# A decoder layer whose side work is placed by an account of the engines' time, with keys in column parts and FFN weight chunks converted on ScalarE

## The chip, the core and the metric

The kernel runs on one core of one Trainium2 chip. A core has TensorE (PE in the profile, its weight loads PEld), VectorE (DVE), ScalarE (ACT), GpSimd (POOL) and SyncE (SP, which here only issues DMAs). The results of matmuls lie in PSUM tiles, from which VectorE and ScalarE read them. The metric is the time of one execution in microseconds on the device. It was 1882.19 us before the change, the median of three runs from 1882.07 to 1885.43.

## What is computed

The input is x of 16 sequences, 256 positions and 512 columns, with a context of the same shape. Three sublayers are added to it in turn, each behind a layer norm:

```python
x = x + mamba2(layernorm(x))       # W_in 512 -> 2048 z + 2048 x + 64 B + 64 C + 32 dt
x = x + xattn(layernorm(x), ctx)   # linear attention over 16 heads
x = x + ffn(layernorm(x))          # 512 -> 2048 (gate, up) -> 512, ternary weights, int8 activations
# mamba2, per head: h[t] = exp(A dt[t]) h[t-1] + dt[t] x[t] B[t];  y[t] = C[t] h[t] + D x[t]
#   x, B, C go through a causal convolution of 4 taps and silu; y * silu(z); RMS norm; @ W_out
# xattn: qh = sigmoid(q wq + bq); kh = sigmoid(ctx wk + bk); vh = ctx wv + bv
#   kv[h] = sum over positions of kh * vh; state = cumsum(kv over heads); (qh * state) @ wo + bo
# ffn: weights rounded to -1, 0, 1 by the mean of their absolute values; activations to 8 bits
```

## The kernel before

The 16 sequences go in 8 pairs. The 2048 inner columns of the mamba sublayer are 16 units of 128 columns (two heads). One pair and one unit make a **slot**; 128 slots follow one another and are written out by hand in a loop over `s`, which interleaves three units: in slot s, unit s is projected, unit s-1 gets its recurrence, unit s-2 its output product. The main instructions of a slot, by tile name and line of the kernel before:

- TensorE: the projection Z (12 matmuls into `pp`, L676) with four transposes `trx` of unit s-1 in its middle (L941), the projection X (12 more `pp`), the recurrence as matmuls `py` of unit s-1 (L961, L968), the output product `po` of unit s-2 (12 matmuls, L1011).
- VectorE: `times_g` on `m` of unit s-1 (L929, L933), two scans into `m` of unit s (L912), three taps of the convolution into `xs` (L693), `y` of unit s-1 (L976, L981).
- ScalarE: eight `xdt` copies (L951), `zs` (L891), `yh` (L987), the start of the convolution `xs` (L897), `sq` (L998), four `m` (L920), silu of `xs` (L906).
- GpSimd: `yl` (L988), which the output product needs, and `ssq` (L999).

Z and X go into two PSUM buffers in turn (pool `ps_p`, tag `proj`). Z is let go by `zs`, X by the last tap.

All else is a **side step** of a generator (a `Task` in the list `beside`): the layer norm of the next pair (`norm_pair`), its time steps dt and decays (`time_steps`, L700 to L775: tiles `sp_*`, `dt`, `da`), its B and C (`states`: `bc`, `bcT`, `pg`, `g`), the context (`context_pair`: `pk`, `kh`, `ptt`, `ptk`; `context_group`: `kv`, `zp`), the attention of pairs already finished (`batch_end`: `q`, `pa`), and the preparation of the FFN weights (`ffn_sums`, `ffn_quantised`: 48 chunks of 128x512, two passes). A slot has eight moments (`POINTS`). A generator yields what its next step needs (engine, microseconds, allowed moments, moments to wait) and `due` lets it go when the moment is allowed and the microseconds given out on that engine since the last reset stay under `room` (2.3 on VectorE, 2.5 on ScalarE, 2.0 on TensorE, 2.5 on GpSimd). Steps that empty a PSUM bank (`leaves`) go in any case.

A side product on TensorE needs a bank (`Banks.take`): at moment 3, between X and `py`, it takes the buffer of Z ("z"); at moment 7, behind `po`, a bank of its own ("own"). With "z" the two buffers change places: the next Z then waits for the last tap of this slot's X, and no longer the next X.

The order of the instructions on each engine is the order in which the program writes them: no scheduler changes it. The same holds for the DMAs on the queues of SP and POOL. Behind the last slot comes the FFN: 32 tiles of 128 rows, 48 matmuls each, with the last batches' attention beside it.

In the context, keys of two batches go through `pk` (four column tiles, L1225), then four matmuls with `kp` stationary and the 16 columns of `pick` moving (L1246), a copy to SBUF (L1250), a tanh (L1253), a scaling (L1255); the sums over positions `ptt` (L1264) are copied (L1270), turned by four matmuls with a 128x32 selection matrix `sel` (L1277) and copied out (L1289, L1293). An FFN chunk is scaled and rounded on ScalarE (L1474), clipped on VectorE (L1476), brought to bfloat16 on GpSimd (L1480) and stored by GpSimd's DMA queue (L1486).

## Time and profile before

| what | value |
|---|---|
| median of three runs | 1882.19 us |
| the profiled execution | 1887.88 us |
| its span, first to last instruction | 1886.1 us |
| granted TensorE clock, mean | 0.986 |
| busy: PE, DVE, ACT, POOL | 95%, 87%, 66%, 36% of the span |
| slots 2 to 17 | from 52 to 260 us |
| slots 18 to 126 | from 260 to 1512 us |
| last slot and FFN | from 1512 to 1886 us |

Each time in the profile is from the span's start. A row gives line, engine, operation, the tiles written and read, and shapes. In the view of waits a row says which engine stood idle in front of which instruction, who released it, and then the sum, the number of times and the longest. In a timeline a row is start, duration, instruction, and in brackets the idle time in front of it.

The slots' limits in the table are starts of the first matmul of a Z in the timeline of TensorE.

### The profile page before, as it was taken

How to read it: one execution, taken by the hardware profiler on the slowest of the kernel's cores; microseconds unless marked ns; L12 is line 12 of the kernel's file. 1: busy time of each engine (PE TensorE's matmuls, PEld its weight loads, DVE VectorE, ACT ScalarE, POOL GpSimd, SP SyncE). 2: the span in 40 equal slices, each digit the busy share in tenths (PEclk: the TensorE clock that was granted, in tenths of full speed). 3: DMA queues.
4: the chain of work that ended last, by engine and by line, in shares of the span. 5: the costliest groups of instructions: out<-in, count | busy, mean ns of one | idle time of the engine just before them, and what ended most of it. 6: DMA issues, size and time to landing. Idle time of an engine off the chain costs nothing.

```text
span 1886.1 us, 30373 instructions
## 1 busy us (share of the span) xinstructions
PE 1786.5 (95%) x10464; PEld 1018.1 (54%) x10464; DVE 1638.2 (87%) x2711; ACT 1248.1 (66%) x2896; POOL 682.2 (36%) x691
## 2 busy tenths in 40 slices
PE   6789999998999998999999999998999989999998
PEld 4445555555556555555555555565656544444443
DVE  6989888777888889888988998989887888999997
ACT  5777666675666666666666666666666557777775
POOL 1233432344434354546454636463533222211000
PEclk8999999999999999999999999999999999999999
DMA  5764776788768777877597879787867734655454
GB/s 163 240 185 136 235 191 174 217 257 223 168 196 270 201 196 235 258 192 191 185 268 211 199 205 252 202 193 186 238 188 213 250 89 99 133 123 130 108 120 95
DMA packets 296933, 358.95 MB, mean 190 GB/s; under 512 B 163765, under 2 KB 197861, under 8 KB 296778
## 3 DMA queue, kind: packets, MB, share of 16 engines
q1 hardware_dynamic: 277962, 296.13, 60.0%
q0 software_dynamic: 18240, 60.84, 9.4%
q8 instruction: 83, 1.36, 0.3%
q14 instruction: 72, 0.59, 0.1%
q10 hardware_dynamic: 576, 0.04, 0.0%
HBM read 279.70 MB, written 39.58 MB: 169 GB/s over the span
## 4 chain that ended last, share of the span: by engine, by line
PE 57%; DVE 25%; DMA 7%; ACT 5%; issue 4%; POOL 2%; SPq 1%; ACTq 0%; POOLq 0%; DVEq 0%
PE pp L676 21%; PE po L1011 11%; PE po_f L1621 5%; PE pg L1579 4%; PE pu L1579 4%; DVE m L912 4%; DVE xs L693 4%; PE py L961 4%; DVE m L929 2%; PE trx L941 2%; DMA w<-w_d 2%; PE py L968 2%; DVE m L933 1%; DVE sp_q L742 1%; DVE y L976 1%
## 5 line engine op out<-in xcount | busy, mean ns | idle before, releaser
L676 PE MATMUL pp<-lnT_h_m,w 128*128 128x512 f16 (+1 forms) x2056 | 661.1, 383 | 23.3 <-DVE xs L693 20.8
L676 PEld LDWEIGHTS <-w 128*128 128x128 f16 x3084 | 296.5, 99 | 364.3 <-issue 35.8
L988 POOL TENSOR_TENSOR yl<-y,yh 128x512 fp32r<-128x512 f32 x128 | 178.9, 1398 | 717.5 <-ACT yh L987 659.3
L693 DVE SCALAR_TENSOR_TENSOR xs<-pp,convw_sb,xs 128x510 f32<-128x510 f32 (+2 forms) x384 | 286.1, 745 | 151.1 <-ACT xs L897 141.6
L676 PE MATMUL pp<-lnT_l_m,w 128*128 128x512 f16 (+1 forms) x1028 | 393.4, 383 | 0.0
L1011 PE MATMUL po<-wout,yh 128*128 128x512 f32 x1024 | 337.0, 410 | 4.6 <-DMA wout<-wout_d 4.6
L951 ACT ACTIVATE xdt<-trx,dt 128x64 f32<-128x64 f32 x1024 | 223.5, 328 | 167.4 <-PE trx L941 167.3
L912 DVE TENSOR_TENSOR_SCAN m<-dab,starts 128x512 f32<-128x512 f32 x254 | 302.2, 1230 | 0.5 <-DMA dab<-da_d 0.5
L1011 PEld LDWEIGHTS po<-wout,yh 128*128 128x128 f32 x1024 | 183.8, 189 | 61.3 <-issue 15.1
L1011 PE MATMUL po<-wout,yl 128*128 128x512 f32 x512 | 203.7, 398 | 3.0 <-POOL yl L988 3.0
L906 ACT ACTIVATE xs<-xs 128x512 f32<-128x512 f32 x128 | 80.9, 632 | 186.3 <-DVE xs L693 186.3
L961 PE MATMUL py<-m,xdt 128*64 128x256 f32 x1024 | 162.1, 395 | 11.1 <-DVE m L933 5.2
L1579 PEld LDWEIGHTS <-yT 128*128 128x128 bf16 x1024 | 100.0, 98 | 131.1 <-issue 14.7
L920 ACT ACTIVATE m<-edb,m 128x128 f32<-128x128 f32 x508 | 162.7, 395 | 12.1 <-DVE m L912 12.1
L999 POOL TENSOR_TENSOR ssq<-ssq,sq 128x512 f32<-128x512 f32 x120 | 158.6, 1321 | 27.9 <-ACT sq L998 27.0
L897 ACT ACTIVATE xs<-pp,convb_sb,convw_sb 128x512 f32<-128x512 f32 x128 | 100.3, 783 | 102.2 <-PE pp L676 102.1
L929 DVE TENSOR_TENSOR m<-m,g 128x1024 f32<-128x1024 f32 x128 | 161.9, 1265 | 0.1
L1579 PE MATMUL pg<-w_ffn,yT 128*128 128x512 bf16 x512 | 132.3, 381 | 4.7 <-ACT h L1583 4.7
L1579 PE MATMUL pu<-w_ffn,yT 128*128 128x512 bf16 x512 | 132.3, 381 | 4.6 <-DVE x L1037 4.6
L1621 PE MATMUL po_f<-w_ffn,hT 128*128 128x512 bf16 x512 | 125.4, 379 | 2.0 <-DMA hT<-hq 2.0
L1583 ACT ACTIVATE h<-pg,sg 128x512 f32<-128x512 f32 x128 | 86.6, 683 | 51.6 <-PE pg L1579 51.3
L1011 PEld LDWEIGHTS po<-wout,yl 128*128 128x128 f32 x512 | 96.7, 189 | 29.7 <-POOL yl L988 6.4
(278 smaller groups left out, 2791.9 us busy)
## 6 DMA issues: line engine op xcount, KB each, us to landing
dab<-da_d SPq DMA_DIRECT2D x127, 512.0 KB
wout<-wout_d SPq DMA_DIRECT2D x112, 512.0 KB
edb<-ed_d SPq DMA_DIRECT2D x127, 256.0 KB
w<-w_d SPq DMA_DIRECT2D x40, 512.0 KB
raw<-in_w_zx SPq DMA_DIRECT2D x16, 512.0 KB
wout_d<-wout SPq DMA_DIRECT2D x16, 512.0 KB
ctxT<-in_ctx_t POOLq DMA_DIRECT2D x16, 512.0 KB, 7.8
x<-in_x SPq DMA_DIRECT2D x16, 512.0 KB
```

The lines of the kernel that those rows point to most:

```text
L676: nc.tensor.matmul(dst, w(wi, kc), yT[yi][:, :, kc, :], start=n == 0, stop=n == 3 * KD - 1)
L693: nc.vector.scalar_tensor_tensor(u[:, :, d:S], raw[:, :, 0 : S - d], w[:, j : j + 1], u[:, :, d:S], ALU.mult, ALU.add,)
L912: nc.vector.tensor_tensor_scan(u["m"][:, 4 * j : 4 * j + 4, :].rearrange("p k t -> p (k t)"), u["da"][j].rearrange("p h i t -> p (h i t)") ...
L920: nc.scalar.activation(u["m"][:, 8 + n, :], u["ed"][:, n // 2, n % 2, :], AF.Copy, scale=u["m"][:, 2 * n, P - 1 : P],)
L929: nc.vector.tensor_tensor(m, m, gi.unsqueeze(2).to_broadcast([P, 2, 2, NT * P]), ALU.mult)
L951: nc.scalar.activation(u["xdt"][:, j, i, h, :], u["tr"][:, j, i, h * HD : (h + 1) * HD], AF.Copy, scale=dt[:, i, j, 2 * c + h : 2 * c + h ...
L961: nc.tensor.matmul(py[h * HD : (h + 1) * HD, j, :].rearrange("p (i t) -> p i t", i=NT), xdt[:, j, 0, h, :], m[:, 2 * (2 * j + h) : 9 + 2 * ...
L988: nc.gpsimd.tensor_tensor(lo, u["y"], hi, ALU.subtract)
L999: nc.gpsimd.tensor_tensor(pair["ssq"], pair["ssq"], sq, ALU.add)
L1011: nc.tensor.matmul(pair["po"][n], u["yhl"][yi][:, j, i * P : (i + 1) * P], w[:, wi, :], start=c == 0 and p == 0, stop=c == NU - 1 and p == 2,)
L1579: nc.tensor.matmul(dst, yT[:, kc, :], w_ffn[w + kc][:, cols], start=kc == 0, stop=kc == KD - 1)
L1621: nc.tensor.matmul(u["po"], u["hT", k // (KF // 2)][:, k % (KF // 2), :], w_ffn[2 * KD + k // NF][:, (k % NF) * D : (k % NF + 1) * D], sta ...
```

## The change

1. **The account.** A `Model` holds one running time per engine. Every main instruction of a slot and every side step adds its microseconds there, behind what it depends on; VectorE steps that read two SBUF tensors and GpSimd steps push each other back. From slot 18 on, `due` no longer goes by `room`: a step goes when its input is ready by the account and `fits` says that the taps (VectorE), the `xdt` copies (ScalarE) or GpSimd's times would not come later than the account has TensorE needing them, plus a slack that grows with the step's delay and, from five slots before its deadline, with its urgency. `Banks.take` asks the same before a side product. Waits between steps of a task are cut to one moment.
2. **Order.** Norm, time steps and states of the next pair but one start one slot earlier (`AHEAD` 4 for 3).
3. **Keys.** `pick` (now 128x32) is stationary and `kp` moves, in four column tiles; the tanh reads PSUM; one transpose (`pk3`) turns the result; the scaling reads it from PSUM. The sums `ptt` are laid out by halves of the columns so that two transposes replace the four matmuls with `sel`; the copies out double. `pg` is two matmuls (256 and 128 columns) instead of three.
4. **FFN chunks.** The copy to bfloat16 is a ScalarE activation; the store stays on GpSimd's DMA queue, at least four moments later.

The diff, cut to its core (the calls `model.op(...)` behind each main instruction, with its microseconds, are left out, and the `us=` given to each `bank.take`):

```diff
+class Model:
+    def __init__(self):
+        self.t = dict.fromkeys(("pe", "act", "dve", "pool"), 0.0)
+        self.port, self.pool = [], []
+        self.proj, self.turn = [0.0, 0.0], 0
+        self.tp = 0.0
+    def op(self, engine, us, *after, port=False):
+        start_ = max([self.t[engine]] + [a + 0.1 for a in after])
+        if port:
+            for a, b in self.pool[-6:]:
+                if a <= start_ < b:
+                    start_ = b
+                    break
+            self.port.append((start_, start_ + us))
+        elif engine == "pool":
+            for a, b in self.port[-8:]:
+                if a < start_ < b:
+                    start_ = b
+                    break
+            self.pool.append((start_, start_ + us))
+        self.t[engine] = start_ + us
+        return start_ + us
+    def bank(self):
+        self.turn = 1 - self.turn
+        return 1 - self.turn
+    def convolved(self, dve, x_end):
+        return max(dve, max(x_end, self.t["act"]) + 0.9) + 2.3
...
+    def urgent(self, task):
+        return 0.5 * max(0, clock[0] / POINTS - task.deadline + 5)
+    def fits(self, task, moment, us):
+        t, e = self.t, task.engine
+        slack = 0.3 + 0.25 * max(0, clock[0] - task.due) / POINTS + self.urgent(task)
+        if e == "dve":
+            if moment < 3:
+                taps = self.convolved(t["dve"] + us, t["pe"] + X_US)
+                end = t["pe"] + X_US + Y_US + OUT_US
+            else:
+                taps = self.convolved(
+                    t["dve"] + us + G_US + SCAN_US, t["pe"] + X_US + Z_US
+                )
+                end = t["pe"] + Z_US + X_US + Y_US + OUT_US
+            return taps <= end + slack
+        if e == "act":
+            return t["act"] + us <= t["pe"] + Z_US / 2 + 0.8 + slack
+        if e == "pool":
+            return t["pool"] + us <= t["pe"] + (5.0 if moment > 3 else 9.0) + slack
+        return True
+Z_US, X_US, Y_US, OUT_US, G_US, SCAN_US = 3.1, 2.6, 1.5, 2.85, 1.9, 2.45
+model = Model()
+current = [None]
+def modelled():
+    return (NU + 2) * POINTS <= clock[0] < NP * NU * POINTS
...
+    def take(self, own=False, first=False, us=None, leaves_us=0.7):
         me = [own]
+        task = current[0]
+        us = us or (task and task.pe_us) or 0.3
         self.line.insert(0 if first else len(self.line), me)
+        asked = clock[0]
+        def fits():
+            if not modelled():
+                return True
+            t, slack = model.t, 0.3 + 0.25 * (clock[0] - asked) / POINTS
+            slack += model.urgent(task)
+            if task.ready > t["pe"] + slack:
+                return False
+            if clock[0] % POINTS == 3:
+                taps = model.convolved(t["dve"], t["pe"])
+                return taps <= t["pe"] + us + Y_US + OUT_US + slack
+            taps = model.convolved(
+                t["dve"] + leaves_us + G_US + SCAN_US, t["pe"] + us + Z_US + X_US
+            )
+            return (
+                self.free_at <= t["pe"] + slack
+                and taps <= t["pe"] + us + Z_US + X_US + Y_US + OUT_US + slack
+            )
         while True:
             moment = clock[0] % POINTS
             if steady() and moment == 3:
                 others = [one for one in self.line if not one[0]]
-                if self.free["z"] and others and others[0] is me:
+                if self.free["z"] and others and others[0] is me and fits():
                     hold = "z"
                     break
             elif self.free["own"] and self.line[0] is me and (
-                not steady() or moment == 7 and clock[0] >= self.since
+                not steady() or moment == 7 and clock[0] >= self.since and fits()
             ):
                 hold = "own"
                 break
             yield WAIT
         self.line = [one for one in self.line if one is not me]
         self.free[hold] = False
+        if task and steady():
+            after = [task.ready]
+            if hold == "z":
+                self.z = model.bank()
+                after.append(model.proj[self.z])
+            else:
+                after.append(self.free_at)
+            task.ready = model.op("pe", us, *after)
...
-        for n, (s0, t0) in enumerate(((0, 0), (P, P), (0, P))):
+        for n, (s0, t0, t1) in enumerate(((0, 0, S), (P, P, S))):
             nc.tensor.matmul(
-                pg[:, n, :], bcT[0:NS, j, s0 : s0 + P], cT[:, j, t0 : t0 + P],
-                start=True, stop=True,
+                pg[:, 2 * n : 2 + n, :].rearrange("p n t -> p (n t)"),
+                bcT[0:NS, j, s0 : s0 + P], cT[:, j, t0:t1], start=True, stop=True,
             )
         yield leaves(dve(0.7))
         nc.vector.tensor_tensor(
-            g[:, j, 0:2, :], pg[:, 0:2, :], upper.unsqueeze(1).to_broadcast([P, 2, P]),
+            g[:, j, 0:2, :], pg[:, 0:3:2, :], upper.unsqueeze(1).to_broadcast([P, 2, P]),
             ALU.mult,
         )
-        nc.vector.tensor_copy(g[:, j, 2, :], pg[:, 2, :])
+        nc.vector.tensor_copy(g[:, j, 2, :], pg[:, 1, :])
...
         yield moved(1.3, 1)
         ct.append(q2.tile([P, NT, D], F32, tag="ctx", name=f"ctx_{b + k}"))
         nc.gpsimd.dma_start(ct[k], cx[b + k].rearrange("(i p) d -> p i d", p=P))
     yield pe(0.2, 1)
-    hold = yield from bank.take()
-    pk = misc(hold, [P, 2, NT, H], f"pk2_{b}")
-    for k in range(2):
-        for i in range(NT):
-            nc.tensor.matmul(
-                pk[:, k, i, :], kp[:, k, i * P : (i + 1) * P], pick, start=True, stop=True
-            )
-    yield leaves(dve(0.1))
-    nc.vector.tensor_copy(kh[:, :, :, 0:H], pk)
-    bank.give(hold)
-    yield act(0.1)
-    nc.scalar.activation(kh[:, :, :, 0:H], kh[:, :, :, 0:H], AF.Tanh, scale=0.5)
-    yield dve(0.1)
-    nc.vector.tensor_scalar(
-        kh[:, :, :, 0:H], kh[:, :, :, 0:H], 0.5, 0.5, ALU.mult, ALU.add
-    )
-    yield pe(0.5)
-    hold = yield from bank.take()
-    pt = misc(hold, [P, D], f"ptt_{b}")
+    hold = yield from bank.take(us=0.35)
+    pk = misc(hold, [P, P], f"pk2_{b}")
     for k in range(2):
         for i in range(NT):
             r = 64 * k + 32 * i
             nc.tensor.matmul(
-                pt[r : r + 32], kh[:, k, i, :], ct[k][:, i, :],
+                pk[r : r + 32], pick, kp[:, k, i * P : (i + 1) * P],
                 start=True, stop=True, tile_position=(0, r),
             )
-    yield leaves(dve(0.6))
-    tt = q1.tile([P, D], F32, tag="ttT", name=f"ttT_{b}")
+    yield leaves(act(0.3, 2))
+    khT = q1.tile([P, P], F32, tag="khT", name=f"khT_{b}")
+    nc.scalar.activation(khT, pk, AF.Tanh, scale=0.5)
+    bank.give(hold)
+    yield pe(0.2, 2)
+    hold = yield from bank.take(us=0.15)
+    pk = misc(hold, [P, 2, NT, 32], f"pk3_{b}")
+    nc.tensor.transpose(pk.rearrange("p k i h -> p (k i h)"), khT, ident)
+    yield leaves(dve(0.1))
+    nc.vector.tensor_scalar(
+        kh[:, :, :, 0:H], pk[:, :, :, 0:H], 0.5, 0.5, ALU.mult, ALU.add
+    )
+    bank.give(hold)
+    yield pe(0.5)
+    hold = yield from bank.take(us=1.0)
+    pt = misc(hold, [P, 2, P], f"ptt_{b}")
+    for i in range(NT):
+        for n in range(2):
+            for k in range(2):
+                r = 64 * n + 32 * k
+                nc.tensor.matmul(
+                    pt[r : r + 32], kh[:, k, i, :],
+                    ct[k][:, i, :].rearrange("p (j n d) -> p n j d", j=2, n=2)[:, n],
+                    start=i == 0, stop=i == NT - 1, tile_position=(0, r),
+                )
+    yield leaves(dve(0.4))
+    tt = q1.tile([P, 2, P], F32, tag="ttT", name=f"ttT_{b}")
     nc.vector.tensor_copy(tt, pt)
     bank.give(hold)
     yield pe(0.2)
     j = b % NG
-    hold = yield from bank.take()
-    pt = misc(hold, [P, KD + 1, 4, 2, 4], f"ptk_{b}")
-    for kc in range(KD):
-        nc.tensor.matmul(
-            pt[:, kc].rearrange("p q k h -> p (q k h)"), tt[:, kc * P : (kc + 1) * P],
-            sel.rearrange("p q k h -> p (q k h)"), start=True, stop=True,
-        )
+    hold = yield from bank.take(us=0.6)
+    pt = misc(hold, [P, 2 * P + 2 * H], f"ptk_{b}")
+    for n in range(2):
+        nc.tensor.transpose(pt[:, n * P : (n + 1) * P], tt[:, n], ident)
+    sums = pt[0:1, 2 * P :].rearrange("p (k q h) -> p k q h", k=2, h=4)
     for k in range(2):
         for i in range(NT):
             nc.tensor.matmul(
-                pt[0:1, KD, :, k, :], ones[:, 0:1],
+                sums[:, k], ones[:, 0:1],
                 kh[:, k, i, 0:H].rearrange("p (q h) -> p q h", h=4),
                 start=i == 0, stop=i == NT - 1,
             )
-    yield leaves(dve(0.2))
-    nc.vector.tensor_copy(
-        group["tt"][:, :, :, j : j + 2, :].rearrange("p c q k h -> p (c q) (k h)"),
-        pt[:, 0:KD].rearrange("p c q k h -> p (c q) (k h)"),
-    )
-    nc.vector.tensor_copy(group["ksum"][:, :, j : j + 2, :], pt[0:1, KD])
+    yield leaves(dve(0.3))
+    turned_ = pt[:, 0 : 2 * P].rearrange("p (c k q h) -> p c k q h", c=KD, k=2, h=4)
+    for k in range(2):
+        nc.vector.tensor_copy(
+            group["tt"][:, :, :, j + k, :], turned_[:, :, k, 0:4]
+        )
+        nc.vector.tensor_copy(group["ksum"][:, :, j + k, :], sums[:, k])
     bank.give(hold)
     ctxs.give()
     paired.add(b)
...
         yield dve(0.5)
         nc.vector.tensor_scalar(t, t, MAGIC + 1.0, MAGIC - 1.0, ALU.min, ALU.max)
         yield from q8s.take()
-        yield pool(1.3)
+        yield act(0.65)
         q = q2.tile([P, 512], BF16, tag="wq8", name=f"wq8_{k}")
-        nc.gpsimd.tensor_scalar(q, t, -MAGIC, None, ALU.add)
+        nc.scalar.activation(q, t, AF.Copy, bias=-MAGIC)
         chunks.give()
+        yield issued()
         if w < 2:
             dst = (wg_d, wu_d)[w][:, n // NF, (n % NF) * 512 : (n % NF + 1) * 512]
         else:
...
 def due(task, now):
     if now < task.due or now % POINTS not in task.points:
         return False
+    if task.engine and task.engine != "dma" and modelled():
+        if task.engine == "pe":
+            if task.ready > model.t["pe"] + 0.3:
+                return False
+            task.pe_us = task.us
+        else:
+            if not task.must and (
+                task.ready > model.t[task.engine] + 0.2
+                or not model.fits(task, now % POINTS, task.us)
+            ):
+                return False
+            task.ready = model.op(task.engine, task.us, task.ready, port=task.port)
+        task.engine = None
+        return True
+    if modelled() and not task.engine and task.ready > model.t["pe"]:
+        return False
+    if task.engine == "pe":
+        task.pe_us = task.us
     if task.engine:
         used = spent.get(task.engine, 0)
         scarce = (first_room if now < (NU + 2) * POINTS else room)[task.engine]
...
+                    task.port = task.engine == "dve" and not must
+                    if modelled() and task.engine and task.engine != "dma":
+                        wait = min(wait, 1)
+                    elif not task.engine and wait > 4:
+                        task.ready = 0.0
...
-    if (s == 1 or c == NU - 3) and k + ahead < NP:
+    if (s == 1 or c == NU - AHEAD) and k + ahead < NP:
         pair = pairs[k + ahead] = {"k": k + ahead}
-        start(s, norm_pair(pair), rank=-4)
-        start(s, time_steps(pair), rank=-1 if k else -5)
-        start(s, states(pair), rank=-1)
+        first = (k + ahead) * NU
+        start(s, norm_pair(pair), rank=-4, deadline=first - 11)
+        start(s, time_steps(pair), rank=-1 if k else -5, deadline=first - 3)
+        start(s, states(pair), rank=-1, deadline=first)
...
-            start(s, batch_end(batches[2 * ended["k"] + j]), rank=2)
+            start(s, batch_end(batches[2 * ended["k"] + j]), rank=2, deadline=s + 12)
```

## The prediction

> **What bounds the kernel now.** I read the page first, for shares; then the starts of the matmuls, slot by slot; then the stretches between slots; then the waits of TensorE inside the slots; last one disturbed place in the timelines.
>
> ```profile
> PE 1786.5 (95%) x10464; PEld 1018.1 (54%) x10464; DVE 1638.2 (87%) x2711; ACT 1248.1 (66%) x2896; POOL 682.2 (36%) x691
> ...
> PE 57%; DVE 25%; DMA 7%; ACT 5%; issue 4%; POOL 2%; SPq 1%; ACTq 0%; POOLq 0%; DVEq 0%
> ```
>
> TensorE is the bound, and VectorE is close enough behind it to hold it up now and then: 25% of the chain that ended last runs through VectorE.
>
> ```profile
> core 0: us, PE busy (x) PEld busy (x) DVE busy (x) ACT busy (x) POOL busy (x), PEclk, DMA share, GB/s
> 0.00:260.00 260.00, 218.92 (x1243) 129.49 (x1244) 222.99 (x367) 169.88 (x397) 77.34 (x94) 0.95 0.65 193
> 260.00:1512.00 1252.00, 1210.52 (x7527) 723.31 (x7523) 1078.12 (x1558) 822.38 (x2160) 554.53 (x539) 0.99 0.77 213
> 1512.00:1886.00 374.00, 357.08 (x1703) 165.30 (x1701) 337.06 (x787) 255.81 (x340) 50.32 (x58) 1.00 0.50 112
> ```
>
> The account works in the second row alone (slots 18 to 126). The first is unmodelled; the last has 1536 FFN matmuls 0.216 us apart, 332 of its 374 us, and the built order of the changed kernel differs there by one late `pa`. So the row to cost is 1252 us, 109 slots.
>
> By the starts of the matmuls a slot with no side product takes 10.08 us (slots 28 to 31, each 10.07 to 10.09): 24 `pp` at 0.216, 12 `po` at 0.235, `py` 1.45, `trx` 0.44. 109 x 10.08 = 1099, so 153 us are on top. The side products at the price of their undisturbed groups: `pk`, `pk2`, `ptt`, `ptk` 1.00, 0.81, 1.08, 1.14, seven times, 28; `bc` with `pd` 3.79, `pda` 0.25, two `pg` 1.93, six times, 36; `kv`, `stp`, `zp` 2.57, four times, 10; `pq` 0.85, six times, 5; `q`, `q_t` and two `pa` 1.24, fourteen times, 17. Together 97. The rest, 56 us, is stall. Of it TensorE's waits in this stretch name 41, these five and six under 1.7:
>
> ```profile
> PE pp L676 <- DVE xs L693: 20.2, 12, 3.4
> PE py L961 <- DVE m L933: 4.6, 5, 1.1
> PE po L1011 <- DMA wout<-wout_d: 4.6, 2, 4.3
> PE trx L941 <- ACT xs L906: 3.3, 4, 1.3
> PE pk L1246 <- DVE kp L1231: 2.4, 1, 2.4
> ```
>
> Half of the named stall is one event twelve times over: Z waits for the last tap of the slot before. Here is the longest:
>
> ```profile
> 1271.97 1.25 DVE L735 TENSOR_SCALAR sp_s<-sp_v 128x128 f32<-128x128 f32 x1
> 1273.25 0.95 DVE L736 RECIPROCAL sp_s<-sp_s 128x128 f32<-128x128 f32 x1
> ...
> 1275.03 2.30 DVE L693 SCALAR_TENSOR_TENSOR xs<-pp,convw_sb,xs 128x510 f32<-128x510 f32 x3
> ```
>
> ```profile
> 1273.55 0.40 PE L1122 MATMUL pa<-z,q 96*128 96x512 f32 x1
> 1277.39 0.39 PE L676 MATMUL pp<-lnT_h_m,w 128*128 128x512 f16 x1 [3.44 <-DVE xs L693]
> ```
>
> Five time-step instructions stood ahead of the taps, and a `pa` in Z's buffer had made the next Z wait for those taps. Either alone does less harm: without the side product Z takes the buffer that `zs` freed and only X, 3.1 us later, needs the taps. The account's `fits` tests exactly this pair.
>
> **The change, part by part.** The sum is made against the profiled execution, 1887.9 us. Two rows of the groups (busy time and mean ns of one behind the bar) price the moved copy: as it is on GpSimd, and the same shape on ScalarE.
>
> ```profile
> L1480 POOL TENSOR_SCALAR wq<-wchunk 128x512 bf16<-128x512 f32 x48 | 77.0, 1604 | 2.9 <-DVE wchunk L1476 2.9
> ...
> L1555 ACT ACTIVATE yq<-y 128x512 bf16<-128x512 f32 x32 | 20.1, 629 | 43.2 <-DVE y L1547 43.2
> ```
>
> *TensorE's own work.* The four `pk2` groups of a pair take 0.81 to 0.89 (eight passes 0.112 apart, and the way out). Four column tiles are shown by `pk` (L1225): its four tiles start 0.007 apart, the rounds of 256 columns 0.195 to 0.22. One round pair of 128 columns is 0.22, plus 0.1 going in (0.31 to 0.33 from the matmul before, where untiled groups have 0.22) and 0.1 going out: 0.42. The new transpose costs 0.26 (`pda`). 0.68 for 0.85: -0.17. `ptk`'s turning goes from eight passes (0.90) to four (0.44 and 0.1 out): -0.36. `ptt` stays: twice the matmuls, half the columns. `pg` loses one weight load and keeps its columns, 0.86 to about 0.78. 8 x 0.53 + 16 x 0.08 = -5.5; bounds 0 (the new handshake PSUM, ScalarE, TensorE, VectorE eats it) and -9 (a round as cheap as the 0.007 spacing suggests).
>
> [...] The trace shows some 0.2 us for going in and out. [...]
>
> *The account.* 41 us of stall are named. The DMA rows (`wout` 4.6, the streamed `w` 1.5) are not its business: 35 left. It is blind in one place that I can price: `time_steps` declares 1.2 us for five instructions that take 0.23 + 0.95 + 0.29 + 0.29 + 0.23, at least 2.0 and in the timeline above 3.1; and 1.7 for nine that take 9 x 0.29 = 2.6, in slot 104 4.7 with GpSimd beside them. That is about 2 us too little, in each of the six pairs from slot 18 on: 12 us that I leave standing. 35 - 12 = -23. Bounds: 0, and -43 (all 35 and half of the 16 unnamed). I take the value nearer the middle since the gaps of over 2 us lie both in time-step slots (56, 72, 89, 104) and elsewhere (34, 40, 57).
>
> *What it adds.* Held to the account, VectorE's side work comes in bundles. From the built order and the rows' medians, slots with over 4 us of it rise from 5 to 14; slots 71 and 88 get 7.6 each (time steps and a norm). A slot frees about 2 us of VectorE (10.1 less 8.1 for scans, taps, products), so such a bundle is late by up to 5.5. What hides it: neither has a side product in Z's buffer, and the slots behind them have 0.2 and 0.7 us. If that cover is gone, see the third rival.
>
> *FFN chunks.* GpSimd loses 48 x 1.60 = 77 us. On VectorE, 14 instructions beside `wq` lasted 4.9 us longer than their quickest kind: at most that comes back. Eight transposes on SP (L652) waited 11.8 us for GpSimd behind `wq`; SP queues the decay loads behind them, but TensorE waited for no `dab`. -1, bounds -5 and 0. ScalarE gains 48 x 0.63 (the row of `yq`, 128x512 f32 to bfloat16, 629 ns): 30 us, on an engine busy 822 of 1252. Behind the new copy queue `xdt` and `zs`, for which `py` and the buffer wait. Main work takes 6.4 of a 10.8 us slot, so 4.4 are free; by the built order five slots exceed that (40, 69, 73, 83, 104), by 3.6 in all, before by none. +3, bounds 0 and 30 (every copy in front of an `xdt` that TensorE needs). The chunk's store stands on GpSimd's queue ahead of `yl`; it is issued half a slot behind the copy, so it finds it done: 0.
>
> *Moved steps.* Norm, time steps and states start a slot earlier, with, for each pair, the loads of x and four transposes, `cT`, and the stores of `da` and `ed`, past one slot's `dab`, `edb` and `wout` on SP. The stores land earlier than needed; a transpose that waits on GpSimd could hold a `wout`: 0, bounds 0 and 4.3 (the `wout` row). The small copies (`kh` two for one, `ttT` half as wide, `tt` and `ksum` doubled) change VectorE by -1 us over all pairs: 0.
>
> Sum: -5.5 - 23 - 1 + 3 = -26.5; 1861.4 against 1887.9, and by 1882.19 / 1887.88 that is **1856** on the median.
>
> **The rivals.** *The account takes nearly all.* Slack hides the undercount too; 43 + 5.5 + 1 go: 1834. For it: most stalls are pairings that it tests. Against: six under-declared steps. *The stalls only move.* The account's clock is not the chip's (GpSimd stretches VectorE's steps, weights and DMAs aren't in it), old stalls go and as many come; 5.5 us of products and little more remain: 1876. For it: the `room` rule already left some 80 of the 109 slots without a stall over 0.3 us. *Bundles on VectorE stall TensorE: slower.* Each of the 14 slots waits for what exceeds 4 us (2 free, 0.9 of side products, 1.1 before Z needs the taps): 22 us by the built order, 3 before. With none of the old stall gone that is +19 - 5.5: 1896. It decides where less than 14 us of old stall goes. Against: eleven of the 14 have a slot with under 1.1 us beside them.
>
> **How the numbers follow.** Forecast 0.47 (1842 to 1872), nearly all 0.15, moved 0.18, bundles 0.20. No change is within 0.2%, 3.8 us, about what a measurement of this kernel can tell. Faster: 0.47 + 0.15 + 0.15 of the third = 0.77; same 0.05; slower 0.18. The range 1830 to 1892 leaves out a few hundredths below and the worse half of the bundles above.
>
> **What would show it.** Right: slots 18 to 126 in some 1226 us; `pp <- xs` under 10; waits left in the slots of `sp_s` and `sp_q`; `wq` rows on ACT at 0.63, none on POOL; `pk2` and `pk3` together 0.7. Wrong: `pp <- xs` at 20 or more, or waits at slots 71 and 88 over 3 us (bundles); `py <- xdt` and `pp <- zs` growing (ScalarE); a span of the first 18 slots other than 260 us.

## The result, and the profile after

The changed kernel takes 1935.79 us (median of 4 runs, 1930.6 to 1939.71) against 1882.86 (4 runs) before: a ratio of 1.027, 95% interval 1.0242 to 1.0297. The forecast was 1856. The page of the changed kernel, the shares of its engines and of the chain that ended last:

```profile
PE 1789.3 (92%) x10456; PEld 1013.2 (52%) x10456; DVE 1626.3 (84%) x2717; ACT 1274.7 (66%) x2944; POOL 602.4 (31%) x642
...
PE 54%; DVE 21%; ACT 8%; DMA 7%; issue 6%; POOL 3%; SPq 1%; ACTq 0%; POOLq 0%; DVEq 0%
```

TensorE is as busy as before (1789 us for 1787) in a longer span. VectorE's part of the chain fell from 25% to 21%; ScalarE's rose from 5% to 8%. The same three stretches as in the prediction (start and end, length, busy time by engine, granted clock, DMA share):

```profile
core 0: us, PE busy (x) PEld busy (x) DVE busy (x) ACT busy (x) POOL busy (x), PEclk, DMA share, GB/s
0.00:261.00 261.00, 215.59 (x1255) 127.51 (x1255) 221.80 (x366) 170.47 (x397) 77.98 (x94) 0.95 0.64 193
261.00:1563.00 1302.00, 1214.36 (x7506) 719.64 (x7499) 1068.60 (x1571) 848.59 (x2209) 473.52 (x490) 0.98 0.74 205
1563.00:1938.00 375.00, 359.34 (x1704) 166.07 (x1702) 335.91 (x782) 255.65 (x339) 50.90 (x58) 0.99 0.50 113
```

All the loss lies in slots 18 to 126: 1302 us for 1252, where 1226 was forecast. TensorE's waits in that stretch (total, times, longest):

```profile
PE pp L785 <- DMA w<-w_d: 11.9, 2, 9.4
PE trx L1060 <- ACT xs L1020: 11.3, 8, 2.4
PE py L1083 <- ACT xdt L1072: 10.7, 2, 8.4
PE py L1083 <- DVE m L1050: 8.8, 5, 3.0
PE pp L785 <- DVE xs L802: 7.5, 5, 3.0
PE pda L864 <- ACT zs L1002: 6.2, 5, 2.5
PE pd L819 <- ACT zs L1002: 5.2, 1, 5.2
```

The wait that the account was forecast to shorten did shrink: `pp <- xs` from 20.2 to 7.5 us. What is new stands behind ScalarE and behind loads. The whole list, added up by the releaser's engine:

| TensorE's waits in slots 18 to 126, us | VectorE | ScalarE | DMA | GpSimd | sum |
|---|---|---|---|---|---|
| before | 27.7 | 7.0 | 6.1 | 0.4 | 41.2 |
| after | 18.7 | 46.6 | 20.9 | 1.4 | 87.6 |

46 of the 50 us are here. Why ScalarE is late, its wait for the FFN chunks says. Who waited for a chunk's tile after, and the time from the load's issue to its landing:

```profile
who waited for it (us, times):
  ACT wchunk L1605: 50.1, 16
  ACT wchunk L1570: 18.6, 10
...
DMA to landing us min/median/max: 2.8/6.4/16.3
```

Before:

```profile
who waited for it (us, times):
  ACT wchunk L1439: 9.6, 5
...
  ACT wchunk L1474: 2.6, 2
DMA to landing us min/median/max: 3.0/6.3/13.0
```

The longest case, slot 81, on three engines. GpSimd issues the load of a chunk, behind a `yl` that had waited for ScalarE and a long step of the norm:

```profile
1028.89 1.28 POOL L1113 TENSOR_TENSOR yl<-y,yh 128x512 fp32r<-128x512 f32 x1 [1.96 <-ACT yh L1112]
1030.14 2.14 POOL L747 TENSOR_TENSOR lnl_m<-ln_m,lnh_m 128x1024 f16<-128x1024 f32 x1
1032.24 0.56 POOL L1332 DMA_DIRECT2D ctxT<-in_ctx_t  x1
1032.79 0.55 POOL L1548 DMA_DIRECT2D wchunk<-in_w_down_t  x1
```

ScalarE comes to the chunk at 1034.15, 1.4 us behind the issue, finds it on its way, and stands there with the slot's own work behind it:

```profile
1033.54 0.61 ACT L1611 ACTIVATE wq<-wchunk 128x512 bf16<-128x512 f32 x1
1045.20 0.81 ACT L1605 ACTIVATE wchunk<-wchunk,magic,wscale 128x512 f32<-128x512 f32 x1 [11.05 <-DMA wchunk<-in_w_down_t]
1045.92 1.73 ACT L1072 ACTIVATE xdt<-trx,dt 128x64 f32<-128x64 f32 x8
```

TensorE, done with X at 1039.3, waits for that `xdt`:

```profile
1047.70 1.12 PE L1083 MATMUL py<-m,xdt 128*64 128x256 f32 x4 [8.36 <-ACT xdt L1072]
```

The waits list names `xdt` there; only ScalarE's own row shows that the root is a load. Of TensorE's seven waits for ScalarE over 2.4 us, five (23 us) end within 4.5 us of the end of such a chunk wait.

The middle landing hardly changed (6.3 us before, 6.4 after); what shrank is the distance from issue to use. With the loads paired in order with ScalarE's steps, ScalarE was free for the step under 6.4 us behind GpSimd's issue for 35 of the 96 chunks (48 in each of two passes), before for 11. It came ahead of the landing 26 times (10 before), 23 of them under 6.4 us behind the issue. The account holds the time of each engine; it holds no time at which a load lands, so for it the chunk step cost 0.65 us on an engine with room.

### The profile page after: what moved, and what is told of

It reads as the page before. It is cut to its first block, busy times and chain, and to the rows that moved or that the text cites. A ratio compares the mean times of both kernels' runs of the same rounds, so it can differ in the third digit from the quotient of the medians.

```text
span 1938.0 us, 30330 instructions
## 1 busy us (share of the span) xinstructions
PE 1789.3 (92%) x10456; PEld 1013.2 (52%) x10456; DVE 1626.3 (84%) x2717; ACT 1274.7 (66%) x2944; POOL 602.4 (31%) x642
## 4 chain that ended last, share of the span: by engine, by line
PE 54%; DVE 21%; ACT 8%; DMA 7%; issue 6%; POOL 3%; SPq 1%; ACTq 0%; POOLq 0%; DVEq 0%
PE pp L785 18%; PE po L1138 11%; PE po_f L1753 5%; PE pg L1711 5%; PE pu L1711 5%; DVE xs L802 4%; PE py L1083 4%; DVE m L1027 3%; ACT xdt L1072 2%; DMA wchunk<-in_w_down_t 2%; DVE m L1046 2%; PE trx L1060 2%; PE py L1090 2%; DMA w<-w_d 1%; DMA ln_m<-in_x 1%
## 5 line engine op out<-in xcount | busy, mean ns | idle before, releaser
L1138 PE MATMUL po<-wout,yh 128*128 128x512 f32 x1024 | 341.6, 415 | 4.2 <-DMA wout<-wout_d 4.2
L1027 DVE TENSOR_TENSOR_SCAN m<-dab,starts 128x512 f32<-128x512 f32 x254 | 306.9, 1249 | 0.7 <-DMA dab<-da_d 0.7
L1083 PE MATMUL py<-m,xdt 128*64 128x256 f32 x1024 | 166.5, 404 | 27.5 <-ACT xdt L1072 14.8
L1036 ACT ACTIVATE m<-edb,m 128x128 f32<-128x128 f32 x508 | 163.4, 398 | 19.7 <-DVE m L1027 19.6
```

The costliest lines, as they stand in the source:

```text
L1027: nc.vector.tensor_tensor_scan(u["m"][:, 4 * j : 4 * j + 4, :].rearrange("p k t -> p (k t)"), u["da"][j].rearrange("p h i t -> p (h i t)") ...
L1036: nc.scalar.activation(u["m"][:, 8 + n, :], u["ed"][:, n // 2, n % 2, :], AF.Copy, scale=u["m"][:, 2 * n, P - 1 : P],)
L1083: nc.tensor.matmul(py[h * HD : (h + 1) * HD, j, :].rearrange("p (i t) -> p i t", i=NT), xdt[:, j, 0, h, :], m[:, 2 * (2 * j + h) : 9 + 2 * ...
L1138: nc.tensor.matmul(pair["po"][n], u["yhl"][yi][:, j, i * P : (i + 1) * P], w[:, wi, :], start=c == 0 and p == 0, stop=c == NU - 1 and p == 2,)
```

## The experiments

Theories: **A**, ScalarE, in order, stands in front of unlanded chunks, and that is the main loss. **B**, the copies' own 30 us on ScalarE. **C**, bundles on VectorE. Later **D**, that any shift of side steps costs, the old order being one good place, and **E**, that each part costs by what it does itself. A slot has eight points at which side steps go; the wait of six points behind a chunk's load is in both kernels. The runs with ten points gave ten also to the two other loads that had six, weights kept and `wout` made in the first sixteen slots; slot 18 then began at 260.2 us (whole change) and 263.3 (before), against 261.3 and 260.1.

**Ten points.** After, with

```diff
-                yield landed(6)
+                yield landed(10)
```

> The kernel after, with ScalarE's step on an FFN chunk put ten points behind the issue of the chunk's load instead of six (a slot has eight points of about 1.45 us). Theory A: ScalarE, which works in order, stands in front of chunk loads that haven't landed (its waits for chunks are 68.7 us after against 12.2 us before), and TensorE waits behind it for the x*dt, silu(z) and x pieces queued there. Then the waits of ScalarE for chunks fall from 68.7 us to under 15, slots 18 to 126 from 1302 to about 1260 us, the time to 1885 to 1900 us. Rival B (the copies' own 30 us on ScalarE): the time stays near 1930, over 1920. Rival C (the account lets too much side work stand on VectorE between two pieces of unit work): also over 1920, with ScalarE's waits for chunks gone and as much idle time of TensorE.

1891.7 us, ratio to before 1.0025 (1.0004 to 1.0046): 44 us less than after. No chunk is waited for. ScalarE now comes to a chunk 9.5 us or more behind its issue. B and C fall as the main cause of these 44 us: the copies stay on ScalarE, and VectorE's order is made by the same account. The stretch and TensorE's waits in it:

```profile
260.00:1512.00 1252.00, 1199.86 (x7505) 710.61 (x7498) 1064.06 (x1569) 846.62 (x2208) 485.87 (x490) 0.99 0.75 213
```

```profile
PE pa L1252 <- DMA z<-z_d: 11.5, 1, 11.5
PE pp L785 <- DMA w<-w_d: 10.1, 2, 7.3
PE py L1083 <- DVE m L1050: 6.7, 6, 1.8
PE pp L785 <- DVE xs L802: 6.2, 8, 1.9
```

By releaser: VectorE 13.6, ScalarE 15.2, DMA 21.6, GpSimd 1.7. VectorE's part is half of what it was before; the largest stalls left over are again loads that came late.

**The account told of loads.** After, with the task of a `landed` step not ready before

```diff
-            return (wait if steady() else soon(4)), range(POINTS), None, 0
+            return (wait if steady() else soon(4)), range(POINTS), "land" if modelled() else None, 0
...
+    if task.engine == "land":
+        task.engine = None
+        task.ready = model.t["pe"] + 10.0
```

> The kernel after, with the account told of loads: a step that waits for a load to land is ready no earlier than 10 us of the account's TensorE time behind the load's issue, for every side step, FFN chunks and others (the chunk loads took 6.4 us in the middle, up to 16.3). Theory A in its wider form (the account places steps by the engines' time and knows nothing of transfers, so that engines stand in front of chunks, of `w`, `z` and `lnT_l_q`): ScalarE's waits for chunks under 15 us, 1865 to 1890 us. If only the chunk steps matter: as with ten points, about 1890. Rival C (VectorE): over 1920.

1897.6 us (1.0063; 1.0045 to 1.008), 38 less than after, with 0.2 us of ScalarE's waits for chunks. The cause is confirmed by another way; the size that A had is missed: `lnT_l_q` (12.3 us) and `w` (8.4) are still waited for, as their users pass no `landed` step.

**Each part undone or alone.**

The first of these edits is on the kernel after (copies back on GpSimd), the second too (no account), the third on the kernel before:

```diff
-                yield act(0.65)
+                yield pool(1.3)
...
-                nc.scalar.activation(q, t, AF.Copy, bias=-MAGIC)
+                nc.gpsimd.tensor_scalar(q, t, -MAGIC, None, ALU.add)
...
-                yield issued()
```

```diff
-            return (NU + 2) * POINTS <= clock[0] < NP * NU * POINTS
+            return False
...
-        AHEAD = 4
+        AHEAD = 3
```

```diff
-                yield pool(1.3)
+                yield leaves(act(0.65))
...
-                nc.gpsimd.tensor_scalar(q, t, -MAGIC, None, ALU.add)
+                nc.scalar.activation(q, t, AF.Copy, bias=-MAGIC)
...
+                yield issued()
```

> The kernel after, with the FFN chunks' copy to bfloat16 given back to GpSimd, its store right behind it on the same queue, as before the change. ScalarE loses 48 x 0.61 = 29.5 us, GpSimd gains 48 x 1.55 = 74 us. Rival B (the copies on ScalarE are what cost): 1890 or less. Theory A (waits for chunk loads): the two other ScalarE steps of a chunk stand where they stood, so the time stays within 15 us of 1936, and ScalarE's waits for chunks over 45 us. Rival C (VectorE): within 10 us of 1936.

1930.8 us (1.0231; 1.0191 to 1.027). B, which had 1890 or less, falls: giving the copies back wins 5 us, less than the two intervals can tell apart. But ScalarE's waits for chunks fell too, 68.7 to 35.1, which A had not expected, so the copy's place must cost in two opposite ways (below).

> The kernel after with the account switched off in every slot, so that side steps go by the old rule of fixed room, and the next pair begun three slots ahead as before; keys in column parts, value sums turned and the copy on ScalarE stay. Theory A and rival C: the account is what costs, so the time falls to the time before or below, 1870 to 1885 us (the keys alone were put at -5.5 us). Rival B: the copies on ScalarE cost here too, 1900 us or more.

1909.6 us (1.0125; 1.0083 to 1.0167): the account costs 26 us on top of the rest, but without it the kernel is still 24 slower than before. Neither A nor C had that; B's 1900 or more fits here, and in the next run.

> The kernel before with one part of the change alone: the FFN chunks' copy to bfloat16 by ScalarE in place of GpSimd, with the store a half slot later (the copy goes at the next of ScalarE's points, whatever room is left). Theory A and rival C: within 6 us of the time before, 1877 to 1889 us (29.5 us of ScalarE work in slots in which it idles a third of the time). Rival B: 1900 us or more.

1920.6 us (1.0175; 1.0133 to 1.0216). A had said no change, B 1900 or more. The tile view of the chunk in this kernel:

```profile
  ACT wchunk L1474: 53.7, 15
  POOL wg_d L1487: 17.9, 5
```

The very wait of the changed kernel, with no account in it: 65.7 us for 12.2, and ScalarE comes to 29 of the 96 chunks under 6.4 us behind the issue, for 11 before. Why the distance shrinks is argued from the program and not shown: the copy on ScalarE frees the chunk's buffer at other points of the slot, so the next load is issued at others; and stores that wait for ScalarE's copies stand in GpSimd's queue, in which the loads stand too.

Two more have one part alone: the kernel before with the new `context_constants` and `context_pair`, and the kernel before with the account, `AHEAD` 4 and the two-matmul `pg`.

> The kernel before with one part of the change alone: keys in four column parts, value sums turned (pk2, pk3, ptt, ptk). In the runs of the whole change TensorE's own work in slots 18 to 126, stalls left out, is 10 to 12 us less than before (the prediction had 5.5). If that is the keys, and nothing new waits: 1870 to 1881 us. Rival: the extra round trip over ScalarE (tanh into khT, then a turning) and the moved steps stall TensorE as much as they save: 1883 to 1895 us, with waits of `pk<-ident,khT` over 8 us.

1926.5 us (1.0199; 1.0176 to 1.0223): the rival's side, and beyond it. TensorE's waits here:

```profile
PE py L961 <- DVE m L933: 9.3, 5, 5.4
PE pk L1251 <- ACT khT L1246: 8.7, 2, 5.3
PE pd L710 <- DMA lnT_h_m<-lnh_m: 7.1, 1, 7.1
```

The new handshake is one of several; a late transpose and VectorE's `m` are others, and neither belongs to the keys.

> The kernel before with one part of the change alone: the account, and the next pair begun four slots ahead; the keys and the copy are as before. The prediction's step: 23 us faster, 1858 to 1868 us. Theory A: the account sets ScalarE in front of unlanded chunks also here (35 us of waits with the account and the copy on GpSimd), 1890 to 1925 us.

1930.9 us (1.0255; 1.0227 to 1.0283): 46 slower than before where the prediction's step said 23 faster. Theory A's range holds, but not by A's reason: ScalarE waits only 19.7 us for chunks (12.2 before). TensorE's waits in slots 18 to 126 are 68.2 us for 41.2: VectorE 28.0, no less than before, ScalarE 23.3, GpSimd 9.0, DMA 7.9.

**The same with ten points**, which takes the waits for chunks out of the comparison.

> The kernel before with the FFN chunks' copy on ScalarE and, in addition, ScalarE's step on a chunk ten points behind the load's issue instead of six. The copy alone cost 34 us, with ScalarE's waits for chunks at 65.7 us against 12.2. Theory A (the copy costs because a chunk's buffer comes free and is loaded again at another time, and ScalarE then stands in front of the load): the waits fall under 10 us and the time to 1880 to 1895. Rival B (29.5 us of ScalarE work, and stores that wait for it in GpSimd's queue): 1905 or more.

1903.6 us (1.0089; 1.0069 to 1.0109): no chunk is waited for, and the time lies between the two ranges. What settles B is the same kernel with the copies on GpSimd (below, 1905.8): under the old rule, with ten points, the copies' place makes no difference that the runs can tell.

> The kernel before with the keys' part of the change and ScalarE's step on an FFN chunk ten points behind the load's issue; no account, copy on GpSimd. Theory A: both kernels lose time at unlanded chunks (12.2 us of ScalarE waits before), so 1865 to 1878 us, below the account's own version with ten points (1891.7), and then the account has given nothing. Rival C': the ten points only repaired what the account broke; here they change nothing, and the time is that of the keys alone.

1915.3 us (1.0157; 1.0137 to 1.0176): not what A had, and 11 below the keys alone, which is not what C' had.

> The account alone, keys and copy as before, with ScalarE's step on a chunk ten points behind the load. Theory A: waits for chunks under 10 us, and 20 to 40 us faster than the account alone. With the prediction's -23 for the account the time would be 1855 to 1870 us; stalls on other loads that the account places too early (`w` 7 us, `z` 11.5 us) leave 1875 to 1890.

1914.7 us (1.0172; 1.0148 to 1.0196): 5.7 us of waits for chunks, but only 16 faster than the account alone, and far from the 1890 that A had at most.

> The kernel after with ten points between a chunk's load and ScalarE's step, and the copy given back to GpSimd: the account and the keys alone, without waits for chunks. It differs from the kernel of keys and ten points under the old rule (1915.3 us) by the account alone, and from the account's kernel with ten points and copies on ScalarE (1891.7) by the copy alone. If the account is worth the 23 us that the prediction gave it: 1885 to 1898 us. If it gives nothing once no chunk is waited for: 1908 to 1922. If the copy on ScalarE costs some 20 us in itself: 1865 to 1878.

1915.9 us (1.0178; 1.0156 to 1.0199): the account adds nothing to the keys (1915.3) as long as the copies are on GpSimd. It differs from the 1891.7 of ten points by the copy alone: 24 us. The scan and the smaller product on VectorE, copies on ScalarE (busy us, mean ns of one):

```profile
L1027 DVE TENSOR_TENSOR_SCAN m<-dab,starts 128x512 f32<-128x512 f32 x254 | 318.4, 1295 | 0.0
L1050 DVE TENSOR_TENSOR m<-m,g 128x512 f32<-128x512 f32 x128 | 97.2, 759 | 0.0
```

and with the copies on GpSimd:

```profile
L1027 DVE TENSOR_TENSOR_SCAN m<-dab,starts 128x512 f32<-128x512 f32 x254 | 323.9, 1315 | 0.0
L1050 DVE TENSOR_TENSOR m<-m,g 128x512 f32<-128x512 f32 x128 | 106.0, 828 | 0.0
```

VectorE is 44 us busier in all (1666.6 for 1622.9), 14 of them in these two rows, and TensorE waits 13.5 us for GpSimd (`ssq`, `yl`) instead of 1.7 and 29.8 for VectorE instead of 13.6.

> The account and the copy on ScalarE with the keys as before, ten points between a chunk's load and ScalarE's step: against the whole change with ten points (1891.7 us) the keys alone differ. If the keys give under the account what they take off TensorE's own work (11 us): 1898 to 1908 us. Theory D (any shift of steps outweighs it): anywhere else in 1885 to 1925.

1912.6 us (1.015; 1.0135 to 1.0165). Without the new keys the whole is 21 slower than with them; that is more than their own work, so part of it is the order. It also differs from the account alone with ten points (1914.7) by the copy alone: there the copies on GpSimd cost 2 us, not 24, though VectorE is again busier with them (1654.7 us for 1624.6).

**Is it the parts or any shift?**

The same edit in both kernels, beside the kernel before with ten points:

```diff
-            if s == NU + 1:
+            if s == NU + 2:
                 tasks = [ffn_sums(n) for n in range(3)] + [ffn_means()]
```

> The kernel before with nothing of the change, only ScalarE's step on an FFN chunk ten points behind its load instead of six. Theory D (the order of steps before stands at a good place, and any shift of side steps brings stalls of its own, 20 us or more, whatever it is for): 1895 to 1925 us, though ScalarE's 12.2 us of waits for chunks go. Theory E (each part of the change costs by what it does itself): 1875 to 1890.

1905.8 us (1.0119; 1.0094 to 1.0143).

> The kernel before with the first pass over the FFN chunks begun one slot later (slot 18 for 17) and nothing else: the same work under the same rules, set down otherwise. Theory D: 1895 to 1925 us. Theory E: within 6 us of the time before, 1879 to 1892.

1893.9 us (1.004; 1.0024 to 1.0055): between the two ranges.

> The kernel after with the first pass over the FFN chunks begun one slot later and nothing else. It tells how far the time after (1935.8 us) is that of one order of steps, and how far the parts' own. Theory A: ScalarE still waits for chunks for 40 to 80 us, and the time is 1915 to 1950. Theory D for the other side (1936 is a bad place by chance): under 1910.

1937.8 us (1.0274; 1.0249 to 1.03), with 73.5 us of ScalarE's waits for chunks.

Two shifts of the kernel before that leave all work as it is cost 20 and 8.5 us: a shift alone can make a good part of what each part cost alone, as D says, and the kernel before seems to stand at a good place of its own rule; two shifts can't show more. The kernel after, in the one shift tried, is as slow as it was, with the same waits. Counted from the kernel before with ten points, the whole change with ten points wins 14 us (1891.7 for 1905.8).

**The rest of the stalls.** What was left at ten points were loads and undeclared costs, mended in three steps:

To the kernel with ten points the first adds half a slot between the load of `z` and the first `pa`, and gives the z_d stores to GpSimd:

```diff
+            yield landed(4)
             for i in range(NT):
                 yield pe(0.3, 1 if i else 3)
...
-                    nc.sync.dma_start(
+                    nc.gpsimd.dma_start(
                         z_d[g][k, c : 8 : 4], t[32 * c : 32 * c + 32].bitcast(F32)
                     )
```

The second has them on SyncE again, with a pause between their two groups of four; the third adds to the second half a slot between the transposes of `lnT_l_q` and `q`, and the time steps' real cost:

```diff
+                if not k:
+                    yield issued()
```

```diff
+            yield landed(4)
             yield pe(0.7)
             hold = yield from bank.take(us=0.65)
...
-            yield dve(1.2)
+            yield dve(2.1)
...
-            yield dve(1.7)
+            yield dve(2.7)
```

> The whole change with ten points between a chunk's load and ScalarE's step, and two more loads seen to: TensorE's first `pa` half a slot later behind the issue of `z`, and the eight stores of z_d issued by GpSimd in place of SyncE, in front of whose `w` load they stood. The two stalls were 11.5 and 7.3 us of 1891.7. If nothing new waits: 1871 to 1880 us, below the time before. If every shift of steps brings other waits: 1885 or more.

1886.1 us (1.0003; 0.9982 to 1.0024): `z` is no longer waited for and `w` for 1.8 us, but GpSimd, issuing the stores, delays `ln_mv_m`, ScalarE waits 6.7 us for it, and TensorE 5.0 behind that.

> The whole change with ten points between a chunk's load and ScalarE's step, the first `pa` half a slot later behind the issue of `z`, and the eight stores of z_d in two groups of four half a slot apart, all on SyncE. With the stores on GpSimd the time was 1886.1, with ScalarE held 6.7 us for `ln_mv_m` behind them and TensorE 5.1 us behind that. If that stall goes and the `w` load is not held: 1874 to 1884 us. If SyncE still holds the `w` load, or other waits come: 1886 to 1895.

1887.5 us (1.0013; 0.9998 to 1.0028): that stall went, `lnT_l_q` came (7.8).

> The whole change with what the runs found mended: ten points behind chunk loads, `z` and `lnT_l_q` used half a slot later, the z_d stores in two groups, and the two VectorE steps of the time steps declared at 2.1 and 2.7 us in place of 1.2 and 1.7. The version without the last two stood at 1887.5 us, with 7.8 us of TensorE's waits for `lnT_l_q` and some 10 us for `py<-m` in the slots in which a pair's time steps stand. If these waits go and nothing new comes: 1870 to 1878 us, faster than before. Theory D: 1883 to 1900.

1873.65 us, ratio to before 0.9946 (0.9929 to 0.9962): 0.5% below the kernel before, 62 us below the changed one, as expected. The stretch of slots 18 to 126, and the longest waits in it:

```profile
263.00:1496.00 1233.00, 1196.95 (x7508) 709.34 (x7500) 1069.92 (x1571) 848.70 (x2209) 484.89 (x490) 1.00 0.76 216
```

```profile
PE pp L785 <- DVE xs L802: 6.8, 7, 1.9
PE pda L864 <- ACT zs L1002: 4.0, 4, 1.2
PE pq L1151 <- DVE y L1099: 3.9, 2, 2.3
```

By releaser: VectorE 19.4, ScalarE 11.8, DMA 2.8, GpSimd 1.8. The slots take 1233 us where the prediction had 1226, and no wait in them is longer than 2.3. It is the best of three such orders, and shifts that changed no work moved the time by 8.5 and 20 us, so the 10.6 us below the kernel before can't be put to any one edit.

## Why the prediction was wrong

*The step that failed* is the FFN chunks' "+3, bounds 0 and 30 (every copy in front of an `xdt` that TensorE needs)". It priced ScalarE's busy time, and that was right: 48 copies at 0.614 us, 0.63 forecast. What ScalarE does while it is not busy was left out. Its waits for chunks went from 12.2 to 68.7 us, TensorE's waits for ScalarE from 7.0 to 46.6, past the upper bound. With ten points between load and step 44 us of the time went; of the 80 between forecast and measurement that is the larger part. The row was in the profile before, 9.6 and 2.6 us under the chunk's tile, and the prediction didn't show it. From issue to landing a chunk of 256 KB took 2.8 us at the quickest in the changed kernel, 6.4 in the middle and 16.3 at the slowest. Six points, by estimate 8.6 to 9.0 us (six eighths of a slot, from 1252 us over 109 slots before and 1302 after), would have covered the middle; but they are a distance in the program's order, and of them 1.4 to 6.3 us were left where most of the waits arose.

*The account, -23.* The second step that failed, and most of the other 36 us: with ten points TensorE's named waits are 52 where the forecast left 18. Of the 41 us named, VectorE's 27.7 became 18.7, and 13.6 once no chunk was waited for; but with the account alone they stayed at 28.0, and the kernel was 46 us slower. The prediction set the DMA rows aside as "not its business" and looked for its blindness "in one place", the time steps. It is blind to every load, and its steps go earlier or later than the old rule's, so loads that had been in time before were not: DMA waits rose from 6.1 to 20.9. The longest, 9.4 us, was for a `w` load that stood behind eight z_d stores on SyncE (issued from 396.4 to 405.7 us, the load at 407.8). The stores belong to the context and not to the steps that *moved steps, 0 (bounds 0 and 4.3)* was about; that term was not tried by itself. The under-declared time steps were real: declared in full, and with `q` half a slot later, they and `lnT_l_q` gave 14 us (1887.5 to 1873.65); the two weren't tried apart.

*GpSimd, -1 (bounds -5 and 0).* Under the old rule it holds: copies on ScalarE against GpSimd are 1903.6 to 1905.8 with ten points, where the sum said +2, and VectorE's busy time differs by 1 to 3 us. In the account's order it was too small for VectorE's work: with the copies on GpSimd VectorE is 30 to 44 us busier in all three pairs, and TensorE waits for GpSimd's own steps. What that is worth in time the runs don't agree on: 24 us, 2 with the keys as before, -5 where chunks are still waited for.

*TensorE's own work, -5.5.* Right in sign. By the starts of the matmuls in the mended kernel `pk2` and `pk3` take 0.36 and 0.11 to 0.20 (0.68 forecast), the turning of `ptk` 0.31 for 0.90 (0.54 forecast), `pg` 0.85 for 0.86 (0.78): some -0.9 a pair for eight pairs and -0.01 for each of sixteen `pg` make -7.4. The 10 to 12 us in the expectations were a coarser count, each matmul's distance to the next against the common distance of its kind. The column tiles of `pk2`, the way in and out included, had been put too high (0.42 for 0.36), the two wider `pg` too low (0.78 for 0.85).

*The rivals.* Bundles on VectorE: 3.5 us of stall behind slot 71, over the 3 that the prediction had set as a sign, and 2.6 behind slot 88; but VectorE's whole part of the waits is 18.7, less than before. The first 18 slots took 261 us, as forecast. "The stalls only move" is the nearest, with its price wrong: 9 us went from VectorE, 55 came elsewhere. The wrong signs that the prediction listed for ScalarE, `py <- xdt` growing and waits behind `zs`, are what the profile shows. Three slips in the prediction's sums move nothing: seven of the waits, not six, lay under 1.7 us, the unnamed stall is 15 of the 56 us, and the first rival's sum gives 1833.

*What is open.* What a part costs alone can't be split from what any shift costs: at ten points the keys alone are +9.5, the account alone +8.9, the copy alone -2.2 against 1905.8, and the three together -14. Why the account alone costs what it does, beyond the waits listed, and why the kernel before stands so well was not tried.

## What to carry to other kernels

Here ScalarE, in order, was as late as the latest load that any of its steps touched: it stood 11.05 us in front of one chunk, and TensorE 8.36 us for the `xdt` behind that. When steps are moved or an operation goes to another engine, compare for each step on it the time from its load's issue to its use with the slowest landing in the trace (in the trace, since a distance in the program's order shrinks when the issuing engine is late, in slot 81 to 1.4 us), and look at the engine's own waits, since TensorE's list named only the innocent step behind (`xdt`). A planner of engine times needs landing times too: told of 10 us for each `landed` step, this one came to 1897.6 us for 1935.8. A part judged alone from a tuned order can pay for the shift of the order as well (two shifts that changed no work cost 20 and 8.5 us), so try harmless shifts of the kernel before, and judge the parts together once the new stalls are mended.

## What the hardware showed unexpectedly

The stall of slot 81 of the changed kernel cost more than its 8.36 us: TensorE's granted clock fell to 0.50. Around it (stretch, length, busy times, granted clock, DMA share):

```profile
1040.00:1041.00 1.00, 0.00 (x0) 0.00 (x0) 0.13 (x1) 0.00 (x0) 0.00 (x0) 1.00 1.58 132
1041.00:1042.00 1.00, 0.00 (x0) 0.00 (x0) 0.00 (x0) 0.00 (x0) 0.00 (x0) 0.84 0.45 144
1042.00:1043.00 1.00, 0.00 (x0) 0.00 (x0) 0.00 (x0) 0.00 (x0) 0.00 (x0) 0.50 1.55 177
...
1051.00:1052.00 1.00, 1.00 (x4) 0.75 (x3) 0.98 (x2) 0.24 (x2) 1.00 (x2) 0.54 0.98 273
1052.00:1053.00 1.00, 1.00 (x6) 0.82 (x5) 0.97 (x2) 1.00 (x3) 0.64 (x3) 1.00 0.87 305
```

The last matmul ended at 1039.3; the granted clock is 1.00 up to 1041.6, 0.50 from about 1041.7 and 1.00 again from about 1051.9, 4.2 us after work began at 1047.7. At 0.50 those 4.2 us are by estimate some 2 us on top of the 8.4; the `py` of that slot took 2.76 us where 1.45 is usual. TensorE idles over 2.4 us 14 times in slots 18 to 126 of the changed kernel, 6 times before. Behind 11 of the 14 and 4 of the 6 the clock falls to 0.50 within 5 us of the idle time's start, behind the others it stays at 1.00. The trace's clock record has 0.50 for 61 us there, 20 before. An estimate of the price: TensorE is busy 1214.4 us there for 1210.5, with some 7 us less of its own work, so the clock took some 11. Behind the idle 2.85 us from 583.22 to 586.07 the clock fell only at 587.7, 1.6 us after work had begun again.

How much busier VectorE is beside GpSimd's copies went with the order, not only with the work: the same 48 copies on GpSimd went with 30 to 44 us more of VectorE's busy time in the account's order (three pairs) and 1 to 3 in the old one (two pairs, such as 1638.2 before and 1634.8 with the copies on ScalarE).
